# Four image layers in one kernel: the second layer as images in turns with its first input loaded early, and the third layer's y transform on the raw image

## The chip, the cores and the metric

The kernel runs on one core of a Trainium2 chip. The core has five engines that work at the same time, each through its own list of instructions and in that order: TensorE (PE; its weight loads are listed as PEld), VectorE (DVE), ScalarE (ACT), GpSimd (POOL) and SyncE (SP), which here issues most of the transfers. Engines wait for one another through semaphores, and for transfers through a small number of "lanes", semaphores that the transfers take in rotation: a transfer that wants a lane waits until the one before it on that lane has landed. The metric is the device time of one launch in microseconds; all times below are in microseconds.

## The reference, cut to what matters

Four layers run on four images of 64 x 64 pixels with 128 channels. Each normalises its input over groups of four channels and adds its result to it:

```python
x = x + selective_scan_block(group_norm(x))   # L0
x = x + fourier_block(group_norm(x))          # L1
x = x + spectral_attention(group_norm(x))     # L2
x = x + window_attention(group_norm(x))       # L3
```

In L0, 16 states per channel are scanned along the pixels in four directions; the sum is layer-normalised, gated and projected. L1 is, per image:

```python
f1 = einsum('bixy,ioy->boxy', rfft(x, axis=-1)[..., :16], cw1)
f2 = einsum('bixy,iox->boxy', rfft(x, axis=-2)[..., :16, :], cw2)
h  = irfft(f1, axis=-1) + irfft(f2, axis=-2)
h2 = relu(h @ ff_w0 + ff_b0) @ ff_w1 + ff_b1
out = layer_norm(h2)
```

L2 normalises each channel's picture (`instance_norm`), makes queries, keys and values from low frequencies of it, and so begins with a Fourier transform in y and x; the queries and keys need only few frequencies. With tokens = s * x + o for the group norm's factors, the transform of the tokens is s times the transform of x, with o added at frequency zero.

## The kernel before, in words

The program is `layer0` to `layer3`, one behind the other; between layers the images lie in HBM (x1, x2, x3). An image in SBUF is a tile of 128 partitions (pixels) x 32 groups of pixels x 128 channels, 2 MB.

**layer0** runs 128 units (image, direction, chunk of 512 pixels) of 16 steps. In a step GpSimd forms `dB` (L673), ScalarE `dA` (L678), VectorE scans (L679), TensorE transposes the states (`pt`, L533), ScalarE copies them out (`hT`, L543) and TensorE multiplies them with the output weights (`yT`, L568). The order on four engines is written out by hand (`manual_schedule`, and a table of slots). A unit's projections are worked out during the unit before it: `xd` (L446) is a copy of the projected rows, read by a store and two matmuls (`dp`, L460); `Ct` (L451) is a copy of others, read by four stores. Both have two buffers. The finished `y` of a direction goes to HBM (L584 onwards), and `after` loads it again (`yf`), with the gate `zf`: aggregation of the layer norm's statistics, normalising (`normed`, seen as L418), transposes `pg` (L401), scaling in ScalarE (L622), the gate on GpSimd (L407), the projection `op` (L412), and the residual add with its store (L421). At the end a loop, `while queue or copied`, drains the last transposes, and the last bands of `after` follow.

**layer1** loads image 0 and then the weights, all at its start; w1, w2 and the images on SP, the smaller weights on ACT. For each image `layer1_image` takes the group norm (transposes `gn_ps` at L60, statistics at L61, then a chain of small operations on VectorE and TensorE up to the factors), then for each of two axes the transform `pu` (L823, 64 matmuls, 8 banks' worth, evacuated with the scale by ScalarE as `U`, L824), one addition to `U` (L830), the mixing `pg` (L838, L839, copied to `G` by VectorE), transposes `pt` (L846, copied to `GT`), and the inverse `ph` (L852, written or added to `hT` by VectorE, L862 and L865). The second axis reads the image in another order of pixels, a second load `xa` in pieces of 512 bytes. The feed-forward then runs in 8 chunks of 512 pixels: `pf` (L872, 4 matmuls, each followed by a ReLU in ScalarE, L873), `po` (L877, 16 matmuls), layer norm on VectorE (L882 to L894), residual add (L896) and store. An image's transform stage ends before its feed-forward begins. All engines' order is left to a scheduler here. The set-up of the third layer's weights (`layer2_weights`) is called behind image 0 and computes on VectorE, with four small matmuls and stores.

**layer2** works on two images at a time, two generators whose pieces are put in order by a planner (`Pace.in_turn`) with an estimate of each engine's time; an operation issued with `aside` set does not move the image's own clock. All its instructions carry line L1067, that of the recording wrapper, so they are told apart by tile. At the front: load `xg`, transposes `pg` with statistics, group norm, the factors spread over all pixels (`so`); then `xg` is scaled in place in four chunks on VectorE (two operations of 128 x 1024 each), each chunk stored to scratch; then the statistics of each channel's picture (`in_st`, 32 operations of VectorE; `in_pm` on TensorE), factors `n_sc`, `n_sf` and their columns `tok_cols`; then the y transform `pu` (32 matmuls, copied to `U` by ScalarE), the x transform `px` (copied by ScalarE to `Xs` with the scale in `tok_cols`), the copies `XG`, the transposes `pT`, and the attention's scores (`Z`, `psc`).

**layer3**, the window attention, isn't touched.

Pools are opened and closed in order, and a later pool's memory may be that of an earlier one, so its first writes wait for the last readers there.

Of the kernel before, what the change touches and what calls it, by code (L numbers as in the profile page):

```python
# [17 lines left out]
P = 128  # L18
Q = 68
# [65 lines left out]
def layer0(sh, A, x_in, x_out, scr):  # L85
# [7 lines left out]
    with ExitStack() as ctx:  # L93
# [28 lines left out]
        xds = [wp.tile([65, CH], F32, name=f"xd{n}") for n in range(2)]  # L122
        for xd in xds:
            nc.vector.memset(xd, 0.0)
            nc.vector.memset(xd[64:65, :], 1.0)
# [12 lines left out]
        zeros = wp.tile([P, WD // P], F32, name="zeros")  # L138
        nc.vector.memset(zeros, 0.0)
# [50 lines left out]
        def opening(bank, steps):  # L190

            waiting = {"dve": [], "act": []}
# [25 lines left out]
            pair = lambda name: tmp.tile([P, 2, CH], F32, name=name, tag="t4", bufs=4)  # L218
            whole = lambda: tmp.tile([P, 2, CH, 4], F32, name="h", bufs=3).rearrange("p s t n -> p (s t n)")
            x = whole().rearrange("p (j d) -> p j d", d=DM)  # L220
            for c in range(NCH):
                nc.sync.dma_start(x[:, 4 * c : 4 * c + 4, :], tiles(x_in(0)[c * CH : (c + 1) * CH, :]))
            for name in ("W00", "W01", "W10", "W11"):
                for g in range(4):
                    nc.sync.dma_start(scr(name)[g].rearrange("(p f) -> p f", p=P), zeros)
# [148 lines left out]

        def after(b, st, later, bands):

            for c in bands:
                yield "l"
                rows = slice(c * CH, (c + 1) * CH)
                y = tmp.tile([P, 4, 2 * P], F32, name="yf", tag="t4", bufs=4)  # L380
                nc.sync.dma_start(y, tiles(scr(f"y2{b % 2}")[rows, :]))
# [38 lines left out]
        def residual(b, rows, xr, op):  # L420
            nc.vector.tensor_tensor(xr, xr, op, ALU.add)  # L421
            nc.sync.dma_start(tiles(x_out(b)[rows, :]), xr)
# [10 lines left out]
        def inputs(k, c, u, par, spare):  # L433

            xd, bd, Wd = xds[c % 2], scr(f"B{(NCH * k + c) % 3}"), scr(f"W{k // 2}{par}")
# [13 lines left out]
            def blocks():  # L449
                Ct = tmp.tile([48, 32, 16], F32, name="Ct")[32:48]  # L450
                nc.scalar.copy(Ct, bank["x"][32:48, :].rearrange("n (a t) -> n t a", t=32))  # L451
                for g in range(4):

                    flat = Wd[g, 496 : 496 + 32 * 127 * 16] if k >= 2 else Wd[g]
                    cells = flat.rearrange("(t m a) -> t m a", t=32, a=16)[:, 0:97:32, :].rearrange("t n a -> n t a")
                    nc.sync.dma_start(cells, Ct[4 * g : 4 * g + 4])
# [89 lines left out]
        def products(G, q, hT):  # L546
# [30 lines left out]
            if G["g"] == 3 and q % 2:  # L577

                y, k = U["y"], U["k"]
                ye = y[:, 2 * e : 2 * e + 2, :]  # L580
                if U["pos"] == 0:
                    nc.scalar.copy(ye, U["yT"][e])
                else:
                    nc.vector.tensor_tensor(ye, ye, U["yT"][e], ALU.add)  # L584
                if k == 2:
                    for r in range(2):
                        nc.vector.bn_stats(U["st"][:, 4 * U["pc"] + 2 * e + r, 0, :], y[:, 2 * e + r, :])
                if q == 3:
                    nc.sync.dma_start(U["dst"](k), y)
# [43 lines left out]
        with tc.manual_schedule(engines=order):  # L633
# [4 lines left out]
            for i, (b, k, c) in enumerate(units):  # L638
# [13 lines left out]
                unit = dict(k=k, pos=pos, rev=rev, pc=pc, u=u, yT=[None, None], started=set(), st=ln_st, dst=dst)  # L652
# [7 lines left out]

                for n in range(NS):
# [74 lines left out]
                elif b == NB - 1 and i % per == 3 * per // 4:  # L736

                    done = [NS * (i + 1 + n) + 8 for n in range(NCH)]
                    sides.append(Side(after(b, ln_st, later, range(NCH - 1, -1, -1)), 8 * 6, done[0], 1, done))
            while queue or copied:  # L740
                transposed()()
# [35 lines left out]
def layer1_weights(sh, A, wp):  # L777
# [3 lines left out]
    nc.scalar.dma_start(w["an"], A["c_an1"])  # L781
    for name in ("w1", "w2"):
        w[name] = wp.tile([P, 16, 2, P], F32, name=name)
        nc.sync.dma_start(w[name], A[name])
    w["ff0"] = wp.tile([P, 4, P], F32, name="ff0")
    nc.scalar.dma_start(w["ff0"], A["ff_w0"].rearrange("i (f k) -> i f k", k=P))
    w["ff1"] = wp.tile([P, 4, P], F32, name="ff1")
    nc.scalar.dma_start(w["ff1"], A["ff_w1"].rearrange("(f k) o -> k f o", k=P))
    w["b0"] = wp.tile([P, 4], F32, name="b0")
    nc.scalar.dma_start(w["b0"], A["ff_b0"])  # L790
    w["rows"] = wp.tile([P, 3, P], F32, name="rows1")
    nc.scalar.dma_start(w["rows"], A["l1_rows"].partition_broadcast(P))
    w["sy"] = wp.tile([P, 256], F32, name="c_sy1")
# [4 lines left out]
def layer1_image(sh, w, pools, x_dram, x_out, x=None):  # L798

    nc = sh.nc  # L800
    big, tmp, small, ps = pools
    if x is None:
        x = big.tile([P, NJ, DM], F32, name="x1")
        load_image(nc, x, x_dram)
    s_, o_ = sh.group_norm(lambda j: x[:, j, :], ps, small, tag="a")
# [3 lines left out]
    hT = big.tile([P, NT], F32, name="hT", bufs=1)  # L809
    for axis in range(2):  # L810
# [3 lines left out]
        else:  # L814
            xa = big.tile([P, NJ, DM], F32, name="xa", bufs=1)
            xv = x_dram.rearrange("(h w2 w1) d -> w1 h w2 d", w1=2, w2=32)
            for q in range(2):
                nc.sync.dma_start(xa[64 * q : 64 * q + 64], xv[q])
        U = tmp.tile([P, 3, 16, 64], F32, name="U1", bufs=1)
        for g in range(NJ // 4):  # L820
# [8 lines left out]
            )  # L829
        nc.vector.tensor_scalar(U[:, 1, 0, :], U[:, 1, 0, :], o8, None, ALU.add)  # L830

        G = tmp.tile([P, 64, 16, 2], F32, name="G1", bufs=1)
        wm = w["w1"] if axis == 0 else w["w2"]
        for g in range(4):
# [5 lines left out]
            nc.vector.tensor_copy(G.rearrange("p l m c -> p m c l")[:, 4 * g : 4 * g + 4], pg)  # L840

        for g in range(4):
# [4 lines left out]
            GT = tmp.tile([P, 4, P], F32, name="GT1")  # L847
            nc.scalar.copy(GT, pt)
            for q in range(0, 4, 2):
# [13 lines left out]
                else:  # L863
                    hv = hv.rearrange("p h w -> p w h")[:, l0 : l0 + 8, :]
                    nc.vector.tensor_tensor(hv, hv, ph, ALU.add)  # L865


    for c in range(NCH):
        h1 = tmp.tile([P, 4, CH], F32, name="h1")
        for f in range(4):  # L870
            pf = ps.tile([P, CH], F32, name="pf", tag="a")
            nc.tensor.matmul(pf, lhsT=w["ff0"][:, f, :], rhs=hT[:, c * CH : (c + 1) * CH], start=True, stop=True)  # L872
            nc.scalar.activation(h1[:, f, :], pf, AF.Relu, bias=w["b0"][:, f : f + 1])  # L873
        po = ps.tile([P, 4, DM], F32, name="po", tag="b")
# [6 lines left out]
        h2 = tmp.tile([P, 4, DM], F32, name="h2")  # L881
# [15 lines left out]
        nc.sync.dma_start(x_out[c * CH : (c + 1) * CH, :].rearrange("(j p) d -> p j d", p=P), xc)  # L897


def load_image(nc, x, x_dram):  # L900
    for q in range(4):
        nc.sync.dma_start(
            x[:, 8 * q : 8 * q + 8, :], x_dram[1024 * q : 1024 * q + 1024, :].rearrange("(j p) d -> p j d", p=P)
        )


def layer1(sh, A, x_in, x_out, l2w, wt):

    tc, nc = sh.tc, sh.nc
    with ExitStack() as ctx:  # L910
        pool = lambda name, bufs, **kw: ctx.enter_context(tc.tile_pool(name=name, bufs=bufs, **kw))
        pools = pool("l1big", 2), pool("l1tmp", 2), pool("l1small", 2), pool("l1ps", 4, space=PSUM)
        wp = pool("l1w", 1)
        x = pools[0].tile([P, NJ, DM], F32, name="x1")
        load_image(nc, x, x_in(0))
        w = layer1_weights(sh, A, wp)
        for b in range(NB):
            layer1_image(sh, w, pools, x_in(b), x_out(b), x if b == 0 else None)
            if b == 0:
                setup = pool("l2set", 1)  # L920
                later = layer2_weights(sh, A, l2w, setup, pools[3], wt)
        return later


def layer2_weights(sh, A, wp, setup, ps, wt):
    nc = sh.nc
    w = {}
# [16 lines left out]

    for name, n0, n1 in (("wqk", 0, 1), ("wvp", 2, 4)):
# [16 lines left out]

    for n in (1, 2):
        m = load(f"mix{n}", [Q, 32], A[f"mix{n}"])
# [3 lines left out]
    def three(name):  # L968
        return load(name, [Q, 32, 16], A[name], setup, nc.scalar)

    pa, pb, vra, vrb, via, vib = map(three, ("pa", "pb", "vra", "vrb", "via", "vib"))
    for re, other, n in ((vra, vrb, 3), (via, vib, 4)):
        nc.vector.tensor_scalar(re, re, qc[:, 2:3], None, ALU.mult)
        nc.vector.scalar_tensor_tensor(re, other, qc[:, n : n + 1], re, ALU.mult, ALU.add)
    row = lambda n: rows[:Q, n].unsqueeze(1).to_broadcast([Q, 32, 16])
# [4 lines left out]
    nc.vector.tensor_tensor(W, W, row(4), ALU.mult)  # L980

    nc.vector.tensor_tensor(vra, vra, row(2), ALU.add)
    nc.vector.tensor_tensor(vra, vra, pa, ALU.mult)
    nc.vector.tensor_tensor(W, W, vra, ALU.add)
    nc.vector.tensor_tensor(via, via, pb, ALU.mult)
    nc.vector.scalar_tensor_tensor(W, via, qc[:, 1:2], W, ALU.mult, ALU.add)
    nc.vector.tensor_scalar(W, W, qc[:, 0:1], None, ALU.mult)

    W2 = setup.tile([Q, 32, 2, 8], F32, name="Wpv2")
    nc.vector.tensor_copy(W2, W.rearrange("p r (h e) -> p r e h", e=2))  # L990
    for g in range(4):
# [4 lines left out]
        nc.sync.dma_start(wt[8 * g : 8 * g + 8].rearrange("r e (h m) -> (r e h) m", m=Q), wr)  # L996

# [8 lines left out]
    qk = load("qk", [P, 3, 11, 16], A["l2_qk"], setup)  # L1006
# [3 lines left out]
    for ra, rb, ia, ib, sw in ((qra, qrb, qia, qib, qsw), (kra, krb, kia, kib, ksw)):  # L1010
# [6 lines left out]
        tt(ia, ia, ib, ALU.add)  # L1017
    for name, (a0, b0), (a1, b1), op, cols in (
# [8 lines left out]
        for c in cols:  # L1027
            tt(w[name], w[name], col(c), ALU.mult)
    w["Wb"] = wp.tile([P, 16], F32, name="Wb")
    tt(w["Wb"], qsb[:, 2], kra[:, 2], ALU.mult)  # L1030
    nc.vector.tensor_scalar(w["Wb"], w["Wb"], sc[:, 2, 3:4], None, ALU.mult)
    return w
# [69 lines left out]
def layer2_image(sh, w, pools, x_in, x_out, scr, wt, parity, beside):  # L1102
# [75 lines left out]
    def dft_y(src):  # L1178

        U = large("U2", [P, 2, 32, 64])  # L1180
        for g in range(NJ // 4):
            pu = ps.tile([P, 4, P], F32, name="pu", tag="a")
            for q in range(4):
                nc.tensor.matmul(pu[:, q, :], lhsT=src[:, 4 * g + q, :], rhs=w["an"], start=True, stop=True)
            nc.scalar.copy(
                U.rearrange("p q r t -> p (q r) t")[:, :, 8 * g : 8 * g + 8],
                pu.rearrange("p j m -> p (j m)").rearrange("p (t k) -> p k t", t=8),
            )
# [65 lines left out]
    yield True  # L1254
    scr_x, scr_y = scr
    for n, c in enumerate(C4):
        xc = xg[:, c, :]
        tt(xc, xc, so[:, 0:1, :].to_broadcast([P, 8, DM]), ALU.mult)
        tt(xc, xc, so[:, 1:2, :].to_broadcast([P, 8, DM]), ALU.add)
        rows = slice(1024 * n, 1024 * n + 1024)  # L1260
        nc.sync.dma_start(scr_x[rows, :].rearrange("(j p) d -> p j d", p=P), xc)
        yield n == 3


    mu, var = yield from token_stats(xg)
# [32 lines left out]
    U = yield from dft_y(xg)  # L1298
# [577 lines left out]
def network(tc, A, out):  # L1876
    nc = tc.nc
    with ExitStack() as ctx:
# [10 lines left out]
        layer0(sh, A, lambda b: A["x"][b], lambda b: x1[b], l0.__getitem__)  # L1889
        l2w = ctx.enter_context(tc.tile_pool(name="l2w", bufs=1))  # L1890
        w2 = layer1(sh, A, lambda b: x1[b], lambda b: x2[b], l2w, wt)
# [186 lines left out]
```

## Time and profile before

| | us |
|---|---|
| three runs | 7838.32, 7832.24, 7831.64 (median 7832.24) |
| the profiled execution, device time | 7839.47 |
| its span, first to last instruction | 7837.7 |
| layer0, to its last scan | 0 to 5713 |
| layer0's last bands, to the end of the last `op` | 5713 to 5747 |
| layer1, from its first `pu` to its last residual add | 5783 to 6284 |
| layer2 | 6285 to 7268 |
| layer3 | 7268 to 7838 |

The mean granted clock of TensorE is 0.962 of full speed. In layer 1 the first `pu` of the four images starts at 5783.15, 5912.11, 6038.01 and 6164.10, and the first `pf` at 5841.55, 5969.41, 6095.49 and 6221.68. The `so` of the first pair's first image is copied just before 6301.13, and `pT` follows at 6379.22; in the second pair these are 6786.54 and 6868.6.

How to read it: busy time is the time in which an engine had an instruction running; with matmuls pipelined their durations overlap, so the busy time of a group is less than count times mean. A wait is put down to the instruction whose end came last before the waiting one started. The chain of waits goes back from the last instruction, at each step to what released it.

### The profile page before, as it was taken

The page shows a single profiled execution, that of the slowest core. Times are in us where ns is not written, and L with a number is a line of the kernel's source. Part 1 is how long each engine was busy: PE and PEld are TensorE (multiplying, and loading weights), DVE is VectorE, ACT ScalarE, POOL GpSimd, SP SyncE. Part 2 cuts the span into 40 slices and gives each one's busy share as a digit, 9 for nine tenths or more (in the row PEclk, how much of TensorE's full clock was granted, in tenths as well). Part 3 has the DMA queues.
Part 4 walks back from the last instruction along what each step waited for, and adds up shares of the span by engine and source line. Part 5 has one row for each costly group of instructions (what it writes and reads, how often), then busy time and mean ns, then how long its engine had stood idle before and what let it go on. Part 6 is the DMA issues. An engine that isn't in the chain of part 4 may idle for free. (4 is left out here: it accounts for less than half of the span.)

```text
span 7837.7 us, 141040 instructions
## 1 busy us (share of the span) xinstructions
PE 6346.8 (81%) x52796; PEld 4010.0 (51%) x52796; DVE 6755.1 (86%) x8112; ACT 6108.1 (78%) x9714; POOL 5634.8 (72%) x2574
## 2 busy tenths in 40 slices
PE   7888888878888877888887777787768968687789
PEld 3544444444455444445554444454457756464556
DVE  7999999999999999999999999999955556646678
ACT  7999999999999998999999999999832323314667
POOL 4989999989999998999999999999910013123233
PEclk8999999999999999999999999999989979788899
DMA  6555556545556554555555545555542142231332
GB/s 173 171 163 175 177 174 173 175 154 175 187 172 185 181 171 166 166 183 174 185 175 173 172 152 189 176 174 181 175 106 51 29 120 70 70 107 37 103 96 81
DMA packets 1326912, 1159.93 MB, mean 148 GB/s; under 512 B 694165, under 2 KB 1120753, under 8 KB 1259282
## 3 DMA queue, kind: packets, MB, share of 16 engines
q1 hardware_dynamic: 1324546, 1149.16, 47.7%
q8 instruction: 416, 6.82, 0.4%
q14 instruction: 270, 2.21, 0.1%
q10 hardware_dynamic: 1680, 1.74, 0.1%
HBM read 956.89 MB, written 189.74 MB: 146 GB/s over the span
## 5 line engine op out<-in xcount | busy, mean ns | idle before, releaser
L679 DVE TENSOR_TENSOR_SCAN h<-dA,state,dB 128x512 f32<-128x512 f32 x4096 | 4920.4, 1266 | 201.0 <-POOL dB L673 79.8
L673 POOL TENSOR_TENSOR dB<-du,Bb 128x1024 f32<-128x1024 f32 x2048 | 4810.6, 2385 | 338.2 <-DVE h L679 210.6
L533 PE MATMUL pt<-ident,h 128*128 128x128 f32 x16384 | 2221.9, 279 | 878.9 <-ACT hT L543 863.1
L678 ACT ACTIVATE dA<-delta,A_neg 128x512 f32<-128x512 f32 x4096 | 2761.7, 697 | 159.2 <-DVE h L679 131.3
L533 PEld LDWEIGHTS pt<-ident,h 128*128 128x128 f32 x16384 | 1811.4, 142 | 1930.6 <-ACT hT L543 1708.0
L543 ACT COPY hT<-pt 128x1024 f32<-128x1024 f32 x2048 | 2080.1, 1016 | 163.0 <-PE pt L533 145.1
L568 PE MATMUL yT<-hT,W 128*32 128x256 f32 x16384 | 1378.9, 409 | 1.1 <-ACT hT L543 0.6
L568 PEld LDWEIGHTS yT<-hT,W 128*32 128x32 f32 x16384 | 455.4, 150 | 340.6 <-issue 328.1
L1067 POOL COPY XG<-Xs 64x9 f32<-64x9 f32 (+2 forms) x44 | 10.8, 293 | 758.6 <-ACT Xs L1067 758.6
L164 PE MATMUL cv<-xn,taps 128*128 128x512 f32 x936 | 527.0, 644 | 2.8 <-DVE delta L469 2.8
L1798 POOL TENSOR_TENSOR S<-S,sm 128x784 f32<-128x784 f32 x128 | 191.2, 1494 | 417.4 <-DVE sm L1796 248.0
L472 POOL TENSOR_TENSOR du<-delta,u 128x1024 f32<-128x1024 f32 x128 | 304.7, 2380 | 79.5 <-DVE delta L469 79.4
L460 PE MATMUL dp<-xd,w_dt 65*128 65x512 f32 x512 | 288.7, 646 | 68.4 <-ACT Ct L451 45.9
L443 PE MATMUL xd_ps<-u,w_x 128*48 128x512 f32 x512 | 250.1, 611 | 21.4 <-DVE e L361 15.8
L1805 ACT ACTIVATE S<-S,mx 128x196 f32<-128x196 f32 x512 | 227.9, 448 | 35.4 <-DVE mx L1832 34.9
L164 PEld LDWEIGHTS cv<-xn,taps 128*128 128x128 f32 x936 | 139.2, 188 | 180.6 <-issue 160.5
L873 ACT ACTIVATE h<-pf,b 128x512 f32<-128x512 f32 x128 | 88.0, 687 | 144.9 <-PE pf L872 144.9
L469 DVE SCALAR_TENSOR_TENSOR delta<-delta,dp 128x512 f32<-128x512 f32 x256 | 170.7, 667 | 4.1 <-ACT delta L466 1.1
L1760 PE MATMUL pt<-ident,S 128*98 128x128 f32 x1024 | 164.9, 285 | 3.5 <-POOL S L1798 2.0
L466 ACT ACTIVATE delta<-delta 128x512 f32<-128x512 f32 x256 | 166.0, 649 | 0.0
L460 PEld LDWEIGHTS dp<-xd,w_dt 65*128 65x128 f32 x512 | 76.5, 188 | 173.2 <-ACT Ct L451 98.8
L1067 POOL TENSOR_TENSOR WX<-wr,Xs 128x544 f32<-128x544 f32 x40 | 57.3, 1434 | 148.4 <-issue 62.1
(369 smaller groups left out, 7039.3 us busy)
## 6 DMA issues: line engine op xcount, KB each, us to landing
Bb<-l_B SPq DMA_DIRECT2D x512, 1024.0 KB
W<-l_W SPq DMA_DIRECT2D x512, 256.0 KB
l_y<-y SPq DMA_DIRECT2D x128, 512.0 KB
u<-l_xr SPq DMA_DIRECT2D x64, 512.0 KB
u<-l_xw SPq DMA_DIRECT2D x64, 512.0 KB
y<-l_y SPq DMA_DIRECT2D x56, 512.0 KB
V<-l_v SPq DMA_DIRECT2D x512, 49.0 KB
y<-l_y SPq DMA_DIRECT2D x80, 256.0 KB
```

The lines of the kernel that those rows point to most:

```text
L164: nc.tensor.matmul(pm, lhsT=taps[:, s, t, :], rhs=xn[:, dy : dy + 8, dx : dx + 64], start=(t == 0), stop=(t == 8),)
L443: nc.tensor.matmul(bank["x"], lhsT=w_x[:, s, k, :], rhs=u[:, s, :], start=(s == 0), stop=(s == 1))
L460: nc.tensor.matmul(bank[s], lhsT=w_dt[:, k, s * P : (s + 1) * P], rhs=xd, start=True, stop=True)
L472: nc.gpsimd.tensor_tensor(du, delta, u, ALU.mult)
L533: nc.tensor.transpose(pt[:, j, s, :], G["h"][:, s, t0 : t0 + 32, :].rearrange("p t n -> p (t n)"), sh.ident)
L543: return lambda: nc.scalar.copy(hT, pt.rearrange("p j s d -> p j (s d)"))
L568: nc.tensor.matmul(U["yT"][e][32 * jo : 32 * jo + 32, qo % 2, :], lhsT=U["Ws"][G["g"]][:, :, 4 * q + j], rhs=hT[:, j, :], start=((e, jo) n ...
L673: nc.gpsimd.tensor_tensor(dB, du, B_now[:, q : q + 1, :].to_broadcast([P, 2, CH]), ALU.mult)
L678: nc.scalar.activation(dA, delta[:, s, :], AF.Exp, scale=A_neg[:, k, s, n : n + 1])
L679: nc.vector.tensor_tensor_scan(h[:, s, :, q], dA, dB[:, s, :], state[:, s, n : n + 1], ALU.mult, ALU.add)
L1798: nc.gpsimd.tensor_tensor(Sv, Sv, U["sm"].unsqueeze(2).to_broadcast([P, 4, 196]), ALU.mult)
L1805: nc.scalar.activation(Sn, Sn, AF.Exp, bias=U["mx"][:, n : n + 1], accum_out=sm[:, n : n + 1])
```

## The change

In layer0:

- `xd` and `Ct` have one buffer each; the `zeros` tile lies in a buffer of another tag, and its memset is issued later.
- a tile for image 0 of layer1 is opened ahead of layer0, on the other end of SBUF, and loaded in four parts by SP during units 116 to 119.
- the last unit's `y` stays in SBUF (`kept`) and isn't stored and loaded.
- the last two bands' stores are issued by ACT instead of SP.
- in the drain, each step is followed by the four transposes and the statistics of one chunk of layer1's image 0; behind the drain the group norm's factors are worked out.

In layer1 the image's function is cut into two generators: `layer1_spectrum` (norm and transforms) and `layer1_feed`. For each image the loop takes one half of a feed chunk of the image before, then some pieces of this image's transform, in 16 turns. SP's order is the program's, the other engines' stays the scheduler's. `pf` of a chunk is issued one chunk ahead. `xa` is requested at the end of the first axis's transform, behind the stores of the image before that were issued until then; the next image is loaded behind the loop of turns. The set-up of the third layer's weights is a generator that runs piece by piece beside image 2, and its loads all go on SP.

In layer2 the y transform takes the raw `xg`; ScalarE's copy to `U` carries the factor s, and o is added to the row of frequency zero. The scaling of `xg` in place is issued beside the transform: chunks 0 and 1 on GpSimd, 2 and 3 on VectorE; `in_st` is counted chunk by chunk behind it.

```diff
-        xds = [wp.tile([65, CH], F32, name=f"xd{n}") for n in range(2)]
+        xd = wp.tile([65, CH], F32, name="xd")
...
-                Ct = tmp.tile([48, 32, 16], F32, name="Ct")[32:48]
+                Ct = tmp.tile([48, 32, 16], F32, name="Ct", bufs=1)[32:48]
...
-                y = tmp.tile([P, 4, 2 * P], F32, name="yf", tag="t4", bufs=4)
-                nc.sync.dma_start(y, tiles(scr(f"y2{b % 2}")[rows, :]))
+                if kept:
+                    y = kept.pop()
+                else:
...
-            nc.sync.dma_start(tiles(x_out(b)[rows, :]), xr)
+            eng = nc.scalar if b == NB - 1 and rows.start <= CH else nc.sync
+            eng.dma_start(tiles(x_out(b)[rows, :]), xr)
...
+                if len(units) - 12 <= i < len(units) - 8:
+                    load_part(nc, ahead["x"], x_out(0), i - len(units) + 12)
...
+            def count():
+                for c in itertools.islice(counted, 1):
+                    pt = psx.tile([P, CH], F32, name="gn_ps", tag="x")
+                    for q in range(4):
+                        nc.tensor.transpose(pt[:, q * P : (q + 1) * P], ahead["x"][:, 4 * c + q, :], sh.ident)
+                    nc.vector.bn_stats(st[:, c, :], pt)
             while queue or copied:
-                transposed()()
+                copy = transposed()
+                count()
+                copy()
+            for c in range(NCH):
+                count()
+            ahead["norm"] = sh.group_scale(st, psx, ahead["pool"], "x", exp_rstd)
```

```diff
+def layer1_feed(sh, w, pools, x, hT, x_out):
+    def first(c):
+        h1 = big.tile([P, 4, CH], F32, name="h1", bufs=2)
         for f in range(4):
             pf = ps.tile([P, CH], F32, name="pf", tag="a")
...
+    h1_next = first(0)
+    for c in range(NCH):
+        h1 = h1_next
+        if c + 1 < NCH:
+            h1_next = first(c + 1)
+        yield
         po = ps.tile([P, 4, DM], F32, name="po", tag="b")
...
+        with tc.manual_schedule(engines=engines):
+            for b in range(NB + 1):
+                out = {}
+                if b < NB:
+                    spectrum = layer1_spectrum(sh, w, pools, x_in(b), x, norm, out)
+                    pieces = 32 + 9 * (norm is None)
+                else:
+                    spectrum, pieces = iter(()), 0
+                turns = 2 * NCH if b > 0 else 1
+                for n in range(turns):
+                    next(fed, None)
+                    for _ in range(pieces * n // turns, pieces * (n + 1) // turns):
+                        next(spectrum)
+                        next(setup, None)
+                for _ in itertools.chain(spectrum, fed):
+                    pass
+                if b < NB:
+                    fed = layer1_feed(sh, w, pools, x, out["hT"], x_out(b))
+                if b == 1:
+                    ahead["close"]()
...
+                    setup = layer2_weights(sh, A, l2w, right, pools["ps"], wt, w2)
+                if b + 1 < NB:
+                    x, norm = pools["big"].tile([P, NJ, DM], F32, name="x1", bufs=2), None
+                    load_image(nc, x, x_in(b + 1))
```

```diff
-    def dft_y(src):
+    def dft_y(src, scale=None, then=None):
...
+            if scale is None:
+                nc.scalar.copy(Ug, pg)
+            else:
+                nc.scalar.activation(Ug, pg, AF.Copy, scale=scale)
+                then(g)
...
-    for n, c in enumerate(C4):
+    st = own([P, NJ, 6], "in_st")
+
+    def scaled(g):
+        if g % 2 == 0:
+            return
+        n = g // 2
+        c = C4[n]
         xc = xg[:, c, :]
-        tt(xc, xc, so[:, 0:1, :].to_broadcast([P, 8, DM]), ALU.mult)
-        tt(xc, xc, so[:, 1:2, :].to_broadcast([P, 8, DM]), ALU.add)
+        eng = nc.vector if n in (2, 3) else nc.gpsimd
+        nc.aside = n not in (2, 3)
+        eng.tensor_tensor(xc, xc, so[:, 0:1, :].to_broadcast([P, 8, DM]), ALU.mult)
+        eng.tensor_tensor(xc, xc, so[:, 1:2, :].to_broadcast([P, 8, DM]), ALU.add)
         rows = slice(1024 * n, 1024 * n + 1024)
         nc.sync.dma_start(scr_x[rows, :].rearrange("(j p) d -> p j d", p=P), xc)
-        yield n == 3
-
-    mu, var = yield from token_stats(xg)
+        nc.aside = False
+        if n > 0:
+            counted(st, xg, range(8 * n - 8, 8 * n))
+
+    U = yield from dft_y(xg, s_, scaled)
+    tt(U[:, 0, 0, :], U[:, 0, 0, :], o_.to_broadcast([P, 64]), ALU.add)
+    counted(st, xg, range(24, 32))
+    yield False
+    mu, var = yield from token_stats(xg, st)
...
-    U = yield from dft_y(xg)
     Xs = own([P, 32, Q], "Xs", tmp)
```

## The prediction

> **What bounds the kernel now.** First the page's head: no engine carries the whole span.
>
> ```profile
> span 7837.7 us, 141040 instructions
> ...
> PE 6346.8 (81%) x52796; PEld 4010.0 (51%) x52796; DVE 6755.1 (86%) x8112; ACT 6108.1 (78%) x9714; POOL 5634.8 (72%) x2574
> ```
>
> VectorE's 86% is an average over four layers, so I cut the span by the work's borders: the first layer; its tail; the gap before the second layer's first y transform; that layer's first transform stage alone, three further images, its last feed-forward alone. Columns are the length, then busy time of PE, PEld, DVE, ACT, POOL, granted clock, DMA share, GB/s.
>
> ```profile
> 0.00:5713.00 5713.00, 4662.38 (x36372) 2741.82 (x36372) 5456.44 (x5266) 5259.44 (x7568) 5189.94 (x2277) 0.99 0.55 174
> ...
> 5713.00:5755.00 42.00, 16.82 (x128) 11.63 (x128) 8.16 (x27) 8.18 (x11) 2.34 (x1) 0.74 0.28 83
> 5755.00:5783.00 28.00, 8.62 (x36) 7.08 (x36) 6.50 (x12) 1.28 (x1) 0.00 (x0) 0.50 1.09 253
> ...
> 5783.15:5841.55 58.40, 50.41 (x354) 46.65 (x354) 35.61 (x79) 13.87 (x25) 0.00 (x0) 0.96 0.61 119
> 5841.55:6221.68 380.13, 340.14 (x2129) 278.31 (x2129) 215.03 (x535) 112.05 (x195) 0.00 (x0) 0.96 0.17 40
> 6221.68:6284.20 62.52, 56.58 (x320) 40.89 (x320) 42.22 (x136) 23.50 (x40) 0.00 (x0) 0.99 0.10 30
> ```
>
> The first layer is VectorE's (5456 of 5713). Between 5713 and 5783 nobody is busy: a chain of waits. The second layer is TensorE's, with 340.14 busy of 380.13. The chain of waits names what ends the gap:
>
> ```profile
> 5728.10 2.94 DMA l_y<-y
> 5731.06 3.78 DMA yf<-l_y
> 5734.96 1.67 DVE yf L418 x4
> ...
> 5743.14 3.80 PE op L412 x16
> ...
> 5747.93 2.49 DMA x<-xr
> ...
> 5751.63 6.74 DMA ff<-in_ff_w
> 5758.39 19.64 DMA x<-x
> 5778.16 1.95 PE gn_ps L60 x8
> ...
> 5783.29 9.52 PE pu L823 x64
> ```
>
> TensorE's waits inside the three images (total, times, longest) show what turns could fill:
>
> ```profile
> PE gn_gm L71 <- DVE gn_mv L69: 13.6, 3, 5.1
> PE pf L872 <- DVE hT L865: 9.0, 4, 2.2
> PE pt L846 <- DVE G L840: 6.6, 6, 1.1
> PE pg L838 <- DVE U L830: 5.8, 6, 1.0
> ```
>
> In the third layer a pair's front is a chain on VectorE: the scaling (L1067 is the wrapper's line, so I read by tile: 8 operations of 1.22 per image), statistics, and only then the y transform `pu`. From the copy of `so` (6301.13) to `pT` (6379.22) it takes 78.1; TensorE is busy 55.0 of them.
>
> ```profile
> 6301.13 1.24 DVE xg L1067
> ...
> 6336.27 9.48 PE pu L1067 x64
> ```
>
> **The change, part by part.** The sum is made against the profiled execution: span 7837.7, device time 7839.47, 7.2 above the median of the three runs (7832.24).
>
> *First input early.* Image 0's load (four DMAs on SP) goes to units 116 to 119 of 128, its eight groups of transposes and `bn_stats` into the drain, its norm behind them. In the drain a cycle lasts 2.25: eight transposes 1.11, eight `yT` matmuls 0.60, so 0.54 idle; four more transposes at 1.11/8 each are 0.55. They fit, barely; if not covered they cost 7 × 0.55 = 3.9. The last unit's `y` stays in SBUF, which removes 2.94 + 3.78, but on VectorE the statistics, the norm (gn_st to `pu`: 3.0), a residual add (0.69) and four aggregations now stand in front of L418: by that order it starts at about 5734.7 instead of 5734.96, a gain of 0.3. From there the chain is unchanged: `op` ends 5746.94 in before, 5746.8 after. Behind it on TensorE stands `pu` directly; the residual's store, the `ff` load, the 19.64 load, `gn_ps` and the norm leave the path. So `pu` starts at 5746.8 instead of 5783.15: **−36.3**. Bounds −38 to −30: drain 3.9 longer, or ScalarE's five weight loads and the last store, issued ahead of the first `U` evacuation, 2.6 late with only four banks to absorb it. On SP, `c_an` and `w1` wait for nothing later than the last `dB` (about 5711; 2 MB at 250 GB/s, 8); `w2` waits for a lane held by the store of band 1, and lands about 5747; needed about 5756 (`w1`) and 5785 (`w2`). `xa` waits for another lane (`ff0` landed, about 5751) and lands about 5765; needed about 5775. Cover: 9 to 38.
>
> *Turns.* Spectrum 0 alone (58.4) and the last feed alone (62.5) stay. Between them lie three phases of 380.13/3 = 126.7, with 340.14/3 = 113.4 of TensorE work and 13.3 idle. In after's order a stalled piece has one half of the other generator's turn behind it: four `pf` or sixteen `po`, 3.5 (a feed chunk takes 7.0). That covers the waits for `U` and `G`, 1.0 and 1.1 each, and of the norm's 5.1 leaves 1.6 and some 0.6 of small ones. The wait for the last `hT` add (2.2) stays: nothing stands between it and the next feed's first `pf`. Left: 4.4, so 117.8 per phase: **3 × −8.9 = −26.7**. Bounds: 113.4 (nothing left, −40) and 126.7 (engines' own queues give it all back, 0). SP is now in program order: `xa` of image b stands behind four stores of image b−1, its 2 MB took 12 to land, and it is needed 2 to 5 later by my reading. That is the thinnest cover here; ten late would undo the phase. The layer 2 setup stood beside images 0 and 1 and cost 2.0 (`pt` behind `W`); beside image 2 it costs about that: 0.
>
> *Border to the third layer.* All eight DMA lanes are now held by stores, so the first `xg` load waits for a store to land, 2.5 by `x<-xr`: **+2.4**.
>
> *y transform on the raw image.* ScalarE's copy becomes an activation with scale: 0.586 for the copy here, 0.581 for the same with scale in L824: 0. `pu(0)` no longer waits for scaling and statistics (6336.27 − 6301.13 = 35). Scaling moves half to GpSimd: its 128x1024 operation takes 2.39 in the first layer, 2.85 here, so two chunks take 4 × 2.85 = 11.4 beside 4 × 1.22 on VectorE. What is late next: VectorE's `in_st` of those chunks waits for GpSimd, and behind it stand image 1's statistics and the columns `tok_cols`, which land about 40.8 after `so` instead of 36.1. ScalarE's `Xs` waits for these. But `pu` (9.5) is long done, so `px(0)` ends some 10 behind the columns (its eight groups took 11.5 in before), at about 51 instead of 56.8, and `pT` comes at about 70.5 instead of 78.1: −7.6. In the second pair (82.1 to `pT`, of which more was statistics) about −11. Behind `pT` the order is the same. Together **−18.6**; bounds −28 (columns no later than now: 4.7 more in each pair) and +5 (their 4.7 unrecovered in one pair, nothing won in the other).
>
> VectorE's operation ran 1.20 to 1.22 beside GpSimd's 2.82 in the `Z` products of this layer, 1.22 without: no slowing of VectorE, 0.4 of GpSimd against 2.39. The Trainium skill, GPSIMD Engine Reference, section "Key points", speaks against this part: GpSimd shares its SBUF interfaces with VectorE, with contention when VectorE's instruction has two SBUF inputs. As an estimate from that page, with the two alternating outright, a GpSimd operation would take 2.39 + 1.22 = 3.6, the two chunks 14.4, and the sum would lose 3 per pair, ending 6 higher. The `Z` rows show 2.82, and I go by them.
>
> *First layer's buffers.* One `xd` and one `Ct` in place of two: in a unit of about 44, `xd` is last read some 7 us after it is written and rewritten a unit later; `Ct`'s stores likewise. Slack about 35: 0. The `zeros` memset now stands behind the first taps: +0.5 (0 to 1).
>
> Sum: −36.3 − 26.7 + 2.4 − 18.6 + 0.5 = −78.7; 7839.5 − 78.7 = 7760.8 for an execution like the profiled one, and less 7.2: about **7754** against the median.
>
> **The rivals.** *Turns bring nothing* (queues stall each other or `xa` comes late): for it, in-order engines and the thin cover; against, ScalarE busy 112 and VectorE 215 of 380. +20 to +27: about 7778.
> *The third layer's front only moves the wait* from `pu` to `tok_cols`: for it, 4.7 later columns; against, `pu` off the chain. +19 to +24: about 7776.
> *The early start fails*, since a weight's memory or lane comes free only after the first layer's last store: for it, the stores and `ff` on one path in before; against, the waits read above. About +36: 7790.
> *Slower: the first layer's single buffers.* The copy into `xd` waits each unit for the store or the matmuls that read the old one, on ScalarE ahead of `dA`, which feeds the scan that bounds the layer. 127 units: it cancels everything from 78.7/127 = 0.62 us per unit, is measurably slower from 0.75, and at 1.0 gives 7754 + 127 = 7881. Against it: the slack of 35.
>
> **How the numbers follow.** Forecast 0.60 (its own range 7735 to 7772), turns 0.13, front 0.12, failed start 0.05, single buffers 0.10. A difference within 0.2% (16 us) can't be told from none. All but the last are faster: 0.90; of the last 0.02 lies within 16 us of before and 0.08 above. The range goes from 7728 (−38, −40 and −28 in place of the three gains) to 7798, behind the failed start.
>
> **What would show it.** The last scan ends near 5713 as before; `pu` starts near 5747 with no stretch at clock .50; further `pf` groups begin every 118; `pT` comes 70 after `so`; `in_st` on VectorE waits for GpSimd's `xg`. Wrong it would be if `U` or `pu` waited for `xa`, `w1` or `w2`, if `dA` waited for `xd`'s copy, or if phases kept 126.

## The result, and the profile after

The changed kernel takes 7779.15 us (median of four runs, 7771.44 to 7782.26) against 7835.28 (7831.64 to 7839.69) for the kernel before beside it: a ratio of 0.9927, 95% interval 0.9909 to 0.9944, so 56 us or 0.7% faster. The forecast was faster, 7754, range 7728 to 7798. The direction and the range hold; of the 78.7 us that the sum promised, 58 came in the profiled execution (span 7779.7 against 7837.7).

The page of the changed kernel, its head:

```profile
span 7779.7 us, 141035 instructions
...
PE 6337.0 (81%) x52796; PEld 3998.2 (51%) x52796; DVE 6747.1 (87%) x8097; ACT 6112.9 (79%) x9715; POOL 5675.9 (73%) x2590
```

No engine's busy time moved by over 50 us of some 6000, and the work is the same. What changed is where engines wait, so the stages tell more than the head. The changed kernel's table of stretches, cut at the same events as that of before, to 0.2 us (last scan, first `pu`, first `pf`, start of the last feed alone, end of its last add; columns as in the prediction's table):

```profile
5716.90:5750.90 34.00, 22.78 (x174) 16.09 (x173) 13.14 (x30) 9.59 (x13) 2.34 (x1) 0.77 0.21 71
5750.90:5807.44 56.54, 48.92 (x355) 44.99 (x354) 26.50 (x38) 13.16 (x24) 0.00 (x0) 0.99 0.56 132
5807.44:6163.58 356.14, 333.04 (x2129) 271.56 (x2129) 217.22 (x585) 113.87 (x196) 0.00 (x0) 0.98 0.23 54
6163.58:6227.54 63.96, 56.31 (x320) 40.82 (x320) 41.88 (x136) 23.63 (x40) 0.00 (x0) 0.97 0.10 30
```

The stretch of 28 us at clock 0.50 is gone. The three phases last 356.1 instead of 380.1 with the same number of matmuls (2129): TensorE's idle time in them fell from 40 to 23, and its busy time from 340 to 333, at a mean granted clock of 0.98 instead of 0.96.

The stages side by side, each from its first event to the next one's, in us; the second profile of before is from the experiments. The times are read to a tenth, so an entry is good to 0.1 and a change to 0.2.

| stage | before | before, again | after | change | predicted |
|---|---|---|---|---|---|
| layer0, to its last scan | 5711.9 | 5706.1 | 5716.9 | +5.0 | +0.5 |
| last scan to layer1's first `pu` | 71.2 | 68.3 | 34.2 | −37.0 | −36.3 |
| first `pu` to first `pf` | 58.4 | 58.3 | 56.3 | −2.1 | 0 |
| first `pf` to the last residual add | 442.0 | 441.8 | 419.4 | −22.6 | −26.7 |
| to the first `so` in layer2 | 17.2 | 16.6 | 19.4 | +2.2 | +2.4 |
| layer2, from there to layer3's first `pq` | 1010.1 | 1010.5 | 1004.7 | −5.4 | −18.6 |
| layer3, to the end | 526.9 | 526.2 | 528.8 | +1.9 | 0 |

So the early input and the turns brought what was said, and the third layer's front brought 13 less. VectorE's timeline of the changed kernel in that front shows where (columns: start, duration, engine, line, operation, out<-in, shapes, count, and in brackets the idle time before and what ended it):

```profile
6254.57 1.65 DVE L1155 BATCH_NORM_STATS2 in_st<-xg 128x6 f32<-128x128 f32 x8 [9.60 <-POOL xg L1155]
6256.14 5.08 DVE L1155 TENSOR_TENSOR xg<-xg,so 128x1024 f32<-128x1024 f32 x2
6261.15 1.63 DVE L1155 BATCH_NORM_STATS2 in_st<-xg 128x6 f32<-128x128 f32 x8
6262.70 2.46 DVE L1155 TENSOR_TENSOR xg<-xg,so 128x1024 f32<-128x1024 f32 x2
...
6283.29 0.35 DVE L1155 RECIPROCAL n_sc<-n_sc 128x32 f32<-128x32 f32 x1 [4.65 <-ACT n_sc L1155]
6283.68 1.20 DVE L1155 TENSOR_SCALAR n_sc<-n_sc,scal 128x32 f32<-128x32 f32 x1
6284.92 0.19 DVE L1155 SCALAR_TENSOR_TENSOR n_sf<-in_pm,n_sc 128x32 f32<-128x32 f32 x1
6285.14 2.16 DVE L1155 TENSOR_SCALAR n_sf<-n_sf,scal 128x32 f32<-128x32 f32 x1
6287.22 2.49 DVE L1155 TENSOR_TENSOR so<-n_sc,tok 128x64 f32<-128x64 f32 x2
6289.63 2.50 DVE L1155 TENSOR_TENSOR so<-n_sf,tok 128x64 f32<-128x64 f32 x2
6292.05 1.63 DVE L1155 BATCH_NORM_STATS2 in_st<-xg 128x6 f32<-128x128 f32 x8
```

and GpSimd's timeline beside it:

```profile
6249.75 10.38 POOL L1155 TENSOR_TENSOR xg<-xg,so 128x1024 f32<-128x1024 f32 x4 [502.30 <-PE pu L1155]
6282.49 9.56 POOL L1155 TENSOR_TENSOR xg<-xg,so 128x1024 f32<-128x1024 f32 x4 [22.35 <-ACT U L1155]
```

Two things are to be seen. The first statistics wait 9.60 at the head of VectorE's queue for GpSimd's first chunk. And while GpSimd scales (6249.75 to 6260.1, 6282.49 to 6292.05), some of VectorE's operations are stretched: the first pair of scalings takes 5.08, the next, behind GpSimd's end, 2.46; two operations and two pairs on the first image's path to `tok_cols` take 1.20, 2.16, 2.49 and 2.50 instead of 0.24, 0.24, 0.35 and 0.35 in before:

```profile
6333.67 0.24 DVE L1067 TENSOR_SCALAR n_sc<-n_sc,scal 128x32 f32<-128x32 f32 x1
6333.95 0.19 DVE L1067 SCALAR_TENSOR_TENSOR n_sf<-in_pm,n_sc 128x32 f32<-128x32 f32 x1
6334.18 0.24 DVE L1067 TENSOR_SCALAR n_sf<-n_sf,scal 128x32 f32<-128x32 f32 x1
6334.33 0.35 DVE L1067 TENSOR_TENSOR so<-n_sc,tok 128x64 f32<-128x64 f32 x2
6334.60 0.35 DVE L1067 TENSOR_TENSOR so<-n_sf,tok 128x64 f32<-128x64 f32 x2
```

GpSimd's four operations of the second group (the second image's chunks 0 and 1) end at 6284.84, 6287.26, 6289.62 and 6292.05; VectorE's four end at 6284.88, 6287.30, 6289.71 and 6292.13. The reciprocal (0.35), the operation with an input in PSUM (0.19) and the statistics (1.63) between them keep their durations. So `tok_cols` starts 47.1 behind the end of `so`'s copy; the prediction had 40.8, and before 36.2.

### The profile page after: what moved, and what is told of

It reads as the page before. It is cut to its first block, busy times and chain, and to the rows that moved or that the text cites. A ratio compares the mean times of both kernels' runs of the same rounds, so it can differ in the third digit from the quotient of the medians.

```text
span 7779.7 us, 141035 instructions
## 1 busy us (share of the span) xinstructions
PE 6337.0 (81%) x52796; PEld 3998.2 (51%) x52796; DVE 6747.1 (87%) x8097; ACT 6112.9 (79%) x9715; POOL 5675.9 (73%) x2590
## 5 line engine op out<-in xcount | busy, mean ns | idle before, releaser
L1155 POOL TENSOR_TENSOR xg<-xg,so 128x1024 f32<-128x1024 f32 x16 | 39.3, 2466 | 636.5 <-PE pu L1155 613.6
```

Of the source, the lines that this page charges most:

```text
L1155: r = f(*args, **kw)
```

## The experiments

"Stage" below is the third layer's, 1010.1 before and 1004.7 after. Executions of one kernel differ by some 15 us (21 runs of before: 7832.78 to 7847.37), and of the 9.9 between the two profiles of before 5.8 lie in the first layer. So small effects are read from stages of the profiles, and totals from ratios. The stage itself repeats: 1010.1, 1010.5 and 1010.0 in the three profiles with the old third layer behind an old second one, 1004.7 and 1006.1 in the two with the changed one. The untouched fourth layer behind it varies more, from 521.6 to 531.9 over all profiles. "Behind `so`" is counted from the end of its copy.

**All scaling on VectorE.**

```diff
-        eng = nc.vector if n in (2, 3) else nc.gpsimd
-        nc.aside = n not in (2, 3)
+        eng = nc.vector
```

> The changed kernel with all four chunks of the scaling on VectorE; the y transform still takes the raw image. In the changed kernel's trace VectorE's operations with two SBUF inputs, and its 32-wide tensor_scalar ones, took up to 2.4 us instead of 0.22 to 1.22 while GpSimd scaled. Sharing theory: each of them waits for the GpSimd operation under way, so without GpSimd no scaling operation of VectorE takes over 1.25, no small one over 0.4, 'so' to 'pT' falls from 76.6 to about 68 to 72 in the first pair although VectorE has 9.8 more work per image, and the kernel gains 5 to 15 us on the changed one (about 7764 to 7774). Rival, GpSimd's help is worth its price: the 9.8 us per image lie on VectorE's chain, 'so' to 'pT' grows to 80 or more and the kernel loses 5 to 15 us (7784 to 7794).

Measured: 7775.04, ratio 0.9917 (0.9904 to 0.9931) where the changed kernel has 0.9927; the intervals overlap, so the gain is read from the stage: 995.1, 9.6 less. No scaling operation took over 1.23, no small one over 0.36. (The work that VectorE takes on is 4 × 1.22 = 4.9 per image, 9.8 per pair, not per image.) But `so` to the first image's `pT` was 78, not 68 to 72. That isn't the rival's price: the first image's columns come earlier (44.7 behind `so` instead of 47.1), and its last `px` ends at 53.1 instead of 60.2. `pT` has no idle time before it; it stands 25 behind that `px` in TensorE's list instead of 16, since the planner now puts more of the second image's work ahead of it. The second image gains: its `TT`, the copy of `pT`, comes at 99.7 instead of 110.9.

**GpSimd's chunks last instead of first.**

```diff
-        eng = nc.vector if n in (2, 3) else nc.gpsimd
-        nc.aside = n not in (2, 3)
+        eng = nc.vector if n in (0, 1) else nc.gpsimd
+        nc.aside = n not in (0, 1)
```

> The changed kernel with chunks 0 and 1 on VectorE and 2 and 3 on GpSimd, the other way round. Order theory: the front lost because the first statistics wait 9.6 us at the head of VectorE's queue for GpSimd's first chunk, with VectorE's own scaling behind them; then this swap takes that wait to under 2, 'so' to 'pT' falls by 6 to 9 in each pair and the kernel gains 10 to 18 us on the changed one. Sharing theory: VectorE's operations are still stretched wherever GpSimd works (sum of the stretch about 10 us per pair), the gain is under 6 us.

Measured: 7803.07, ratio 0.9953 (0.9940 to 0.9965), stage 1024.7: slower than the changed kernel, which neither theory had. The head wait did go (3.90 is left, for `pu`), and the norm's small operations are no longer stretched (0.24 at most); what is left of the stretch is an addition to `U` of 0.79 in the first pair, and in the second two of 1.85 and 0.79 and one scaling of 3.41. What replaced them is order: in TensorE's list the second image's `in_pm` stands ahead of the first image's `pT`, as in the changed kernel, but here it waits, and behind it now come all eight groups of the second image's `px` instead of two:

```profile
6305.61 1.06 PE L1155 MATMUL in_pm<-in_st,tok 128*128 128x32 f32 x4 [4.99 <-DVE in_st L1155]
...
6334.80 0.53 PE L1155 MATMUL pT<-ident,XG 64*128 64x64 f32 x5
```

That `in_pm` waits 4.99 for statistics of GpSimd's late chunks, and `pT` comes 82 behind `so` instead of 77, though the first image's last `px` ends at 48 instead of 60. The planner places the pieces by its own estimates, so an edit here moves more than its own cost; this run doesn't separate the two theories.

**GpSimd's operations cut in four.**

```diff
-        eng.tensor_tensor(xc, xc, so[:, 0:1, :].to_broadcast([P, 8, DM]), ALU.mult)
-        eng.tensor_tensor(xc, xc, so[:, 1:2, :].to_broadcast([P, 8, DM]), ALU.add)
+        m = 8 if n in (2, 3) else 2
+        for a, op in enumerate((ALU.mult, ALU.add)):
+            for j in range(0, 8, m):
+                xj = xc[:, j : j + m, :]
+                eng.tensor_tensor(xj, xj, so[:, a : a + 1, :].to_broadcast([P, m, DM]), op)
```

> The changed kernel with each of GpSimd's scaling operations of 128x1024 cut into four of 128x256. If VectorE waits for the end of the GpSimd instruction under way (sharing by whole instructions), the small VectorE operations that took 1.2 to 2.4 fall under 0.9, the pair of scaling operations that took 5.08 falls to about 3.5, and the kernel gains 2 to 8 us. If the two engines share by bandwidth, the durations stay (2.2 to 2.5 for the small ones) and the time stays within 4 us, or grows by the 24 extra instructions' overhead.

Measured: 7768.37, ratio 0.9906 (0.9893 to 0.9920), stage 990.2: 14.5 less than the changed kernel, though GpSimd's own work grew (0.73 per quarter, 13.3 instead of 10.4 from start to end for the first image). VectorE's timeline at the place shown above:

```profile
6291.52 0.45 DVE L1155 TENSOR_SCALAR n_sc<-n_sc,scal 128x32 f32<-128x32 f32 x1
6292.00 0.19 DVE L1155 SCALAR_TENSOR_TENSOR n_sf<-in_pm,n_sc 128x32 f32<-128x32 f32 x1
6292.23 0.42 DVE L1155 TENSOR_SCALAR n_sf<-n_sf,scal 128x32 f32<-128x32 f32 x1
6292.57 1.49 DVE L1155 TENSOR_TENSOR so<-n_sc,tok 128x64 f32<-128x64 f32 x2
6293.98 1.44 DVE L1155 TENSOR_TENSOR so<-n_sf,tok 128x64 f32<-128x64 f32 x2
```

The same operations beside the same elements on GpSimd, but each now waits at most for a piece of 0.73. With shares of a bandwidth the durations would have stayed; VectorE waits for the whole GpSimd instruction under way. The four small steps take 3.80 instead of 8.35, and the shorter pieces also let the statistics start group by group (the head wait is 5.56). Up to `pT` the planner's order is no rival here: from the end of the first image's last `px` to `pT` it is 16.4 in both pairs, as in the changed kernel, and `pT` comes 7.1 and 8.0 earlier, 15.1 together, about what the stage gained.

**The third layer's part undone.** The old order of scaling, statistics and y transform in the changed kernel.

```diff
-    U = yield from dft_y(xg, s_, scaled)
-    tt(U[:, 0, 0, :], U[:, 0, 0, :], o_.to_broadcast([P, 64]), ALU.add)
-    counted(st, xg, range(24, 32))
-    yield False
-    mu, var = yield from token_stats(xg, st)
+    mu, var = yield from token_stats(xg)
...
+    U = yield from dft_y(xg)
     Xs = own([P, 32, Q], "Xs", tmp)
```

> The changed kernel with the third layer's part undone: scaling on VectorE first, then statistics, then the y transform on the scaled image, ScalarE copying without a factor. It tells what that part brought alone. By the traces' stages (5 us of the second pair, none of the first) it loses about 5 us on the changed kernel, 7781 to 7789 for executions like the profiled one. By the prediction's term it would lose 18.6 (7798).

Measured: 7791.05, ratio 0.9934 (0.9921 to 0.9948), stage 1014.0. Against the changed kernel's stage, the part brought 9.3; against before's own 1010, 5.4. The 18.6 of the sum are excluded by the stage; the totals (0.9934 and 0.9927) have overlapping intervals.

**The first layer's buffers alone.** The kernel before with one `xd`, one `Ct` and the moved `zeros`.

```diff
-        xds = [wp.tile([65, CH], F32, name=f"xd{n}") for n in range(2)]
+        xd = wp.tile([65, CH], F32, name="xd")
...
-                Ct = tmp.tile([48, 32, 16], F32, name="Ct")[32:48]
+                Ct = tmp.tile([48, 32, 16], F32, name="Ct", bufs=1)[32:48]
```

> The kernel before with only the first layer's buffers changed: one xd, one Ct, and the zeros tile in another tag's buffer with its memset behind the first taps. The last scan began at 5711.9 in the profile of before and at 5716.9 to 5725.4 in the five profiles of changed kernels. Theory, the single buffers cost: the last scan comes 5 us or more later than in a profile of before taken beside it, and the time grows by 5 to 10 us (7837 to 7842 where before has 7832). Rival, it is only the spread between executions: the last scan of the two differs by the first scan's 1.7 us at most, no ScalarE copy into xd or Ct waits, and the time stays within 3 us.

Measured: 7841.87 against 7839.44, ratio 1.0001 (0.9992 to 1.0010). The last scan began at 5716.8, the first at 113.2; before has 5711.9 and 111.8.

**Before, once more**, with no edit.

> The kernel before once more, for a second profile. Spread theory: its last scan begins anywhere from 5710 to 5726, and the stages behind the first layer last as in the first profile within 1 us each. Theory of the single buffers: its last scan begins near 5712 again.

Measured: one execution, 7829.6; last scan 5706.1, first scan 110.6. All stages behind it are within 1 us of the first profile but one: last scan to `pu` is 68.3 instead of 71.2. In no profile does a copy into `xd` or `Ct` wait for the readers of the one before it; what ScalarE's `xd` copy waits for is the projection, in the buffers run:

```profile
ACT xd L445 <- PE xd_ps L442: 12.4, 21, 3.0
```

and in before:

```profile
ACT xd L446 <- PE xd_ps L443: 10.3, 21, 2.9
```

(total, times, longest). So no cost of the single buffers shows in the total (the interval leaves room for at most 8 us). The first scan is 1.3 to 2.5 later in the buffers run, which fits the moved memset. But all eight profiles with these buffers begin the last scan at 5715.7 to 5725.4, and both without them earlier (5706.1 and 5711.9), so a few us of the +5.0 may be real; from what, no run here tells.

**The turns undone.**

```diff
-                for n in range(turns):
-                    next(fed, None)
...
+                for _ in fed:
+                    pass
+                for _ in spectrum:
+                    next(setup, None)
```

> The changed kernel with the turns undone: an image's feed-forward is written out whole before the next image's transform begins, the early first input and the third layer's part kept. Theory (the turns fill TensorE's waits): from the first pf to the next image's first pf it takes 126 to 127 again instead of 115 to 122, and the second layer is 20 to 26 us longer. Rival (the gain came from requesting xa and the next image earlier, or from pf a chunk ahead, and the scheduler fills the waits by itself): the period stays under 121, and the second layer is less than 8 us longer.

Measured: 7825.30, ratio 0.9985 (0.9975 to 0.9994). From the first `pf` to the last residual add it takes 462.9, 43.5 more than the changed kernel: the theory's direction, but beyond its 20 to 26. The first `pf` of the four images starts at 5811.54, 5938.21, 6084.40 and 6211.15: periods of 126.7, 146.2 and 126.8, where the turns have 115.2, 122.4 and 118.6 and before had 126.7 on average. The early request of `xa` and of the next image changes nothing by itself; the turns do. The middle period is longer than expected by 19.5: it is the one with the weights' set-up beside it.

```profile
PE pw L1077 <- DVE Wpv L1074: 14.7, 1, 14.7
```

TensorE stands 14.7 behind a transpose of the set-up that waits for VectorE. Most of the rest is TensorE's own busy time, 116.2 at a mean clock of 0.91 in this period, 112.5 and 112.7 at 0.96 in the other two. With turns no such wait shows; that the feed's pieces fill it is the likely reason, not shown by a run of its own.

**Only chunk 0 on GpSimd, in quarters.** The findings on the front joined.

```diff
-        eng = nc.vector if n in (2, 3) else nc.gpsimd
-        nc.aside = n not in (2, 3)
+        eng = nc.gpsimd if n == 0 else nc.vector
+        nc.aside = n == 0
...
+        m = 2 if n == 0 else 8
```

> The changed kernel with only chunk 0 scaled on GpSimd, in pieces of 128x256, and chunks 1 to 3 on VectorE. Sharing theory: GpSimd works some 6 us less per image, so no small operation of the norm is stretched, and the third layer's stage is at or below the 990 us of the split kernel (1004.7 in the changed one, 995.1 with all on VectorE). Rival (what counts is the planner's order of the pieces, which moves with every such edit): the stage lies anywhere from 985 to 1015, without relation to the stretch of VectorE's operations.

Measured: 7755.22 (7753.68 to 7758.62), ratio 0.9893 (0.9879 to 0.9906), stage 980.1: the fastest of all, 30 below before in this stage. `pT` of the first image comes at 66.

```profile
6248.87 3.04 DVE L1155 TENSOR_TENSOR xg<-xg,so 128x1024 f32<-128x1024 f32 x2 [5.93 <-PE pu L1155]
6251.84 1.63 DVE L1155 BATCH_NORM_STATS2 in_st<-xg 128x6 f32<-128x128 f32 x8
6253.39 2.46 DVE L1155 TENSOR_TENSOR xg<-xg,so 128x1024 f32<-128x1024 f32 x2
...
6279.35 0.31 DVE L1155 TENSOR_SCALAR n_sc<-n_sc,scal 128x32 f32<-128x32 f32 x1
```

VectorE now waits only for `pu` to have read the chunk (5.93), and then works on up to the second image's statistics; the first image's norm is hardly stretched but for 1.50 in place of 0.35 at one pair of operations (in the second pair of images 0.88 and 0.90 at two). From the end of the first image's last `px` to `pT` it is again 16.4 in both pairs, so up to there the order has no share in the gain: `pT` comes 10.8 and 11.4 earlier than there, 22.3 of the stage's 24.6. Further on in the stage a share of the order isn't excluded. The stage went 1004.7, 995.1, 990.2, 980.1 as the stretch and the head wait went.

## Why the prediction was right, and where it was short

*First input early* (−36.3): measured −37.0, and −34.1 against the second profile of before. The order read for the drain held: the four added transposes fit into its idle time (a cycle is 2.25 before and after), L422 starts 22.4 behind the last scan's start where L418 had 23.1, and from there the chain is the same (8.2 to the start of the last `op` in both).

*Turns* (−26.7, with a period of 117.8): the three periods are 115.2, 122.4 and 118.6, 118.7 on average, −24.0 together; with the first transform stage (−2.1, by the norm taken in the drain) and the last feed (+1.4) it is −24.7. The thin cover of `xa` held. The nearness of 118.7 to 117.8 is in part luck, as two misses cancel. The sum left 4.4 idle per phase beside 113.4 busy; measured are 7.0, 9.2 and 7.0 idle beside 108.2, 113.2 and 111.6 busy. Idle is more because `pt` still waits for `G`, 3.1 per phase, and `pg` once for `U`, 1.0, which the sum had as covered; the waits named as left are there, 2.2 for `hT` in each phase and 2.6 for `gn_d` in the middle one. Busy is less because the granted clock is higher, 1.00, 0.96 and 0.97 where before has 0.95, 0.96 and 0.96; the sum kept before's busy time. Without the turns 0.96, 0.91 and 0.96 come back, with 112.5, 116.2 and 112.7 busy. So the phases lost about 17 of idle time, and about 7 of busy time with the higher clock.

*Border* (+2.4): +2.2. The wait is the one that was named: SP's first `xg` load waits 1.8 for a store `x<-x` to land.

*y transform on the raw image* (−18.6): −5.4. This is the step that failed, in its size. The prediction's words were "no slowing of VectorE", from the `Z` products, where VectorE's 1.20 stood beside GpSimd's 2.82. That row was misread, and before's own trace shows it. GpSimd's `Z` operation takes 2.93 with VectorE's beside it from its start, and 1.90, not 2.39, where none is:

```profile
6380.38 1.20 DVE L1067 TENSOR_TENSOR Z<-TT,W 128x1024 f32<-128x1024 f32 x1
...
6380.42 2.93 POOL L1067 TENSOR_TENSOR Z<-TT,W 128x1024 f32<-128x1024 f32 x1 [20.40 <-DVE TT L1067]
...
6414.21 1.90 POOL L1067 TENSOR_TENSOR Z<-TT,W 128x1024 f32<-128x1024 f32 x1 [18.93 <-DVE TT L1067]
```

So there GpSimd was the one that waited, 0.9 to 1.1 each time (its stretched operations all end 1.76 or 1.77 behind VectorE's end, also the one at 6869.87, whose recorded start is 0.03 ahead of VectorE's). In the front GpSimd was long under way, and VectorE waits. The Trainium skill's sentence that was weighed and set aside (GPSIMD Engine Reference, section "Key points": contention with VectorE's instructions in a 2-port mode or with two SBUF inputs) names the operations with two SBUF inputs, which were stretched here (those of 128x64 by 2.1 us), and not the one with an input in PSUM, which was not. The `tensor_scalar` operations from SBUF to SBUF have one input tensor and were stretched by 1.0 and 1.9; whether they ran in a 2-port mode no row here shows. The price worked out from the page, 6 us on GpSimd's own operations, was not the one paid: these took 2.34 to 2.41 but for one of 3.20 in each pair, less than the 2.85 assumed. VectorE's small operations paid, 7.2 us on the way of the first image to `tok_cols` (1.20 + 2.16 + 2.49 + 2.50 against 1.18), the same again in the second pair of images, with 2.6 more at the first scaling.

What came of it: the columns start 47.1 behind `so` instead of the sum's 40.8; the first image's last `px` ends at 60.2, where the sum had 51 and before 56.8; `pT` comes at 76.6 and 76.8 in the two pairs, where the sum had 70.5 and about 71 and before 78.1 and 82.1. So up to `px` the first image's chain became longer, not shorter. What was won was won behind it, where less TensorE work stands ahead of `pT` (16 instead of 21 and 24).

*First layer* (+0.5): +5.0 in this pair of profiles, a part of it perhaps real. The buffers alone gave a ratio of 1.0001; the rival that put its price there is excluded at any size that could matter (it needed 0.62 us per unit, and 8 us over 127 units are 0.06).

The measured 7779 lies inside the stated range, but outside the 7735 to 7772 that the prediction gave to its own account. Of the rivals, "the front only moves the wait to `tok_cols`", given 0.12, is the nearest to what happened, through a mechanism that it didn't name; its figure was 7776. (The range's lower end, worked out as the prediction says, is 7729 to 7730 rather than 7728.)

## What to carry to other kernels

Before work is given to GpSimd beside VectorE, look at what VectorE runs in the same stretch: here small operations each waited for a whole GpSimd instruction, up to 2.4 us. In each pair that cost 7.2 on a chain of small operations and 2.6 at the scaling, as much as the 9.8 of work that was taken off VectorE. Short GpSimd instructions, placed where VectorE is waiting anyway, keep the gain (here one chunk of four, cut in quarters, gave 30 us where two whole chunks gave 5). And when a row of the trace is used against such a rule, compare each of the two operations with the same operation alone: that tells which of them waited.

## What the runs showed of the hardware that was not expected

The granted clock of TensorE fell to half behind waits of only 2.2 us. The changed kernel's windows at the start of the second and the third feed, cut where the clock steps:

```profile
5922.69:5926.10 3.41, 3.41 (x4) 1.44 (x5) 0.70 (x4) 0.69 (x1) 0.00 (x0) 0.50 0.33 58
5926.10:5932.00 5.90, 5.90 (x20) 2.92 (x19) 0.78 (x6) 4.62 (x7) 0.00 (x0) 1.00 0.41 128
6045.57:6048.98 3.41, 3.41 (x6) 1.32 (x5) 0.00 (x0) 1.37 (x2) 0.00 (x0) 0.50 0.00 0
6048.98:6054.50 5.52, 5.52 (x20) 2.84 (x19) 0.19 (x1) 4.07 (x7) 0.00 (x0) 1.00 0.00 0
```

TensorE is busy through all four; the fall begins 0.05 and 0.6 behind the end of the 2.2 wait for `hT`. The sixteen first `pf` take 8.83 there, and 7.13 in the first and the last feed, where the clock stays at 1.00 behind the same wait: 1.7 more, half of 3.41. A mean clock between 0.50 and 1.00 over a longer window (0.82 over 5922.60 to 5932.00) is here an average of such pieces. Why the clock fell behind two of these four waits and not behind the others, no run here tells.
